# Last layer of a four-layer graph network on one core: where two transposes stand among a block's products, and which block's sum a block's gathers wait for

## The chip, the cores and the metric

The kernel runs on one core of a Trainium2 chip. The metric is device time in microseconds (us) of one execution. The engines are PE (TensorE), DVE (VectorE), ACT (ScalarE), POOL (GpSimd) and SP (SyncE); DMA transfers are issued from SP, ACT and POOL.

## The reference: what is computed

Four graph layers run on 2708 nodes with 128 features, each as `x = layernorm(x + layer(x, adj))`, with one adjacency matrix of a few entries in each row. Only the last layer matters here:

```python
s = x @ msg_w[:, :D].T
d = x @ msg_w[:, D:].T
messages = gelu(s[:, None, :] + d[None, :, :] + msg_b)      # 2708 x 2708 x 128
aggregated = einsum('ijd,ij->id', messages, adj)
new = concat([x, aggregated]) @ upd_w.T + upd_b
h = gelu(new) + x
x = layernorm(x + layernorm(h) * ln_w + ln_b)
```

A message counts only where the adjacency has an entry. For a node i the sum therefore runs over its few neighbours j, and each of them needs row j of `d`.

## The kernel before

**Until the last layer.** The first three layers end with `TD` in DRAM, which holds the rows of `d` by node, and with lists that give each node its neighbours, sorted by degree. The nodes stand in 22 blocks of 128 (the last has 20). The change touches nothing of this.

**One block of the last layer.** A block has up to nine slots of neighbours. Six "pure" slots hold a neighbour for each of the 128 rows; three joined slots pack the rarer further neighbours of several rows together. The block with the 20 last nodes, block 21, has two slots in all. The functions, in `sparse_path`:

- `gathers(k)` (lines 1462 to 1479), on POOL: one indirect DMA for each slot (line 1467) brings 128 rows of `TD` into a tile `G`. Pure slots read their indices from `LP`, joined ones from `LM`, those of block 21 from `LT_`. There are four tiles `G`, used in turn (`ROWS`, line 1145).
- `terms(k)` (1481 to 1496): PE transposes the block's features and places them in the block's order, with two instructions into the PSUM tile `xT_ps` (1484 and 1485). ACT copies that to `xT` (1487), PE makes `sd_ps` (1489), DVE adds the bias to give `S` (1491), and PE spreads `S` to the joined slots as `q_ps` with JOIN products (1495).
- `weights(k)` (1498 to 1513), on DVE: ten tiles `W` of adjacency values.
- `messages(k)` (1515 to 1548): DVE adds `G` to `q_ps` and `S` (1539, 1542), and ACT takes the gelu (1546, 1547), giving `M`.
- `update(k)` (1550 to 1572), on PE, all from line 1557: products of the bias and of `xT`, then the **sum**, ten products `M` by `W` into one half of `af_ps`. ACT copies the sum to `aT` (1567). A last product of `aT` with `UB`, called the copy's product below, goes to the other half. ACT takes the gelu into `yo` (1572).
- `added(k)` and `norms(i)` (1579 to 1631), mostly on DVE: the residual, the two layer norms, and the store of the result from SP. `norms` runs once for a set of one to four blocks (`SETS`, 1388).

**The order.** `pinned` chains each instruction to the one before it on its engine, so every engine runs in the order in which the code emits. `ORDER` (1391) lists the blocks; block 21 stands eleventh, with index 10. The loop (1649 to 1667) goes over `ORDER`. In step n it emits the gathers and terms of block n+1, the messages of block n, the weights of block n+2, the update of block n, the residual of block n-1, and, when a set is full, its norms.

**The hold.** Since a gather needs only indices and a free tile, POOL could run far ahead. `HOLD = {0: 3}` (1460) makes the first gather of the block with index n, for n of 3 or more, wait for the instruction that `updated` names for the block three places back. `product` sets `updated[k]` at every call (1559), so it names the last one, the copy's product:

```python
if j in HOLD and n >= HOLD[j]:
    tc.add_manual_dep(
        i.ins, updated[ORDER[n - HOLD[j]]], ...
```

Of the kernel before, what the change touches and what calls it, by code (L numbers as in the profile page):

```python
# [25 lines left out]
F32 = mybir.dt.float32  # L26
# [11 lines left out]
P = 128  # L38
# [80 lines left out]
def sparse_path(  # L119
# [30 lines left out]
    NB = -(-N // P)  # L150
# [39 lines left out]
    ident = part["ident"]  # L190
# [20 lines left out]
    for h in range(HEADS):  # L211
        k = slice(h * HD, (h + 1) * HD)
# [49 lines left out]
    V_, S_, T_, G_ = nc.vector, nc.scalar, nc.tensor, nc.gpsimd  # L262
    newest = {}

    def pinned(i):

        e = i.ins.engine
        if e in newest:
            tc.add_manual_dep(
                i.ins, newest[e].name,  # L270
                mybir.DependencyInfo(mybir.DependencyClass.NoSync, mybir.DependencyReason.DATA),
                reason="order",
            )
        newest[e] = i.ins
        return i
# [102 lines left out]
    with (  # L378
# [49 lines left out]
        t = ps.tile([P, BANK], F32, name="tr_ps")  # L428
# [3 lines left out]
        t = ps.tile([P, 4, D], F32, name="hw_ps")  # L432
# [13 lines left out]
        t = ps.tile([P, BANK], F32, name="tr_ps")  # L446
# [5 lines left out]
        t = ps.tile([P, 4, D], F32, name="hw_ps")[:, 0, :2]  # L452
# [264 lines left out]
    with (  # L717
# [234 lines left out]
        def weights(k):  # L952
            pinned(S_.activation(HS[:, k, :], HS[:, k, :], AF.Copy, scale=DS[:, k : k + 1]))
# [162 lines left out]
    PLACE = late.tile([P, NB, P], F32, name="PLACE")  # L1116
    PLACE = late.tile([P, NB, P], F32, name="PLACE")
# [6 lines left out]
    X3 = late.tile([P, NB, D], F32, name="X3")  # L1124
# [55 lines left out]
    with (  # L1180
# [16 lines left out]
        t = ps.tile([P, BANK], F32, name="tr_ps")  # L1197
# [148 lines left out]
        for t in ROWS:  # L1346
            n = NG - WHOLE
# [43 lines left out]
    ORDER = [b for bs in SETS for b in bs]  # L1391
    with (
# [52 lines left out]
        def slots(k):  # L1445

            if k == NB - 1:
                return range(NT)
            if k == LAST:
                return (*range(PURE - 1), *range(PURE, NG), PURE - 1)  # L1450
            return range(NG)

        def source(k, s):

            if k == NB - 1:
                return LT_[:, s : s + 1]
            return LP[:, k, s : s + 1] if s < PURE else LM[:, k, s - PURE : s - PURE + 1]

        updated = {}
        HOLD = {0: 3}  # L1460

        def gathers(k):
            n = ORDER.index(k)
            G = Gs[k] = ROWS[ORDER.index(k) % len(ROWS)]
            for j, s in enumerate(slots(k)):
                bound = {"bounds_check": NP - 1, "oob_is_err": False} if s >= WHOLE else {}
                i = G_.indirect_dma_start(  # L1467
                    G[:, s, :], None, TD, bass.IndirectOffsetOnAxis(ap=source(k, s), axis=0),
                    **bound,
                )  # L1470
                if j in HOLD and n >= HOLD[j]:
                    tc.add_manual_dep(
                        i.ins, updated[ORDER[n - HOLD[j]]],
                        mybir.DependencyInfo(
                            mybir.DependencyClass.Sync, mybir.DependencyReason.DATA
                        ),
                        reason="no further ahead of the updates",
                    )
                pinned(i)

        def terms(k):

            t = ps.tile([P, 2 * P], F32, name="xT_ps")
            pinned(T_.transpose(t[:, :P], X3[:, k, :], ident))
            pinned(T_.matmul(t[:, P:], X3[:, k, :], PLACE[:, k, :], start=True, stop=True))
            xT = sb.tile([P, 2 * P], F32, name="xT")
            pinned(S_.copy(xT, t))
            m = ps.tile([P, 2 * D], F32, name="sd_ps")
            pinned(T_.matmul(m, xT[:, P:], W3[:, : 2 * D], start=True, stop=True))  # L1489
            S = sb.tile([P, 2 * D], F32, name="S")  # L1490
            pinned(V_.tensor_tensor(S, m, MB, ALU.add))  # L1491
            js = range(NM, NM + NT) if k == NB - 1 else range(NM)
            q = ps.tile([P, NM, D], F32, name="q_ps")
            for i, j in enumerate(js):
                pinned(T_.matmul(q[:, i, :], JOIN[:, j, :], S[:, :D], start=True, stop=True))  # L1495
            mids[k] = S, q, xT
# [18 lines left out]
        def messages(k):  # L1515
            S, q, xT = mids[k]
            G = Gs.pop(k)
            M = Ms[k] = wp.tile([P, NG + 1, D], F32, name="M")
            if k == LAST:
                last = PURE - 1  # L1520
                pinned(S_.activation(M[:, NG, :], S[:, D:], AF.Gelu))
                pinned(V_.tensor_tensor(
                    M[:, :last, :], G[:, :last, :],
                    S[:, :D].unsqueeze(1).to_broadcast([P, last, D]), ALU.add,
                ))
                pinned(S_.activation(M[:, :last, :], M[:, :last, :], AF.Gelu))
                yield
                pinned(V_.tensor_tensor(M[:, PURE:NG, :], G[:, PURE:, :], q, ALU.add))
                pinned(S_.activation(M[:, PURE:NG, :], M[:, PURE:NG, :], AF.Gelu))
                yield  # L1530
                pinned(V_.tensor_tensor(M[:, last, :], G[:, last, :], S[:, :D], ALU.add))
                pinned(S_.activation(M[:, last, :], M[:, last, :], AF.Gelu))
                return
            if k == NB - 1:
                n = NT
                pinned(V_.tensor_tensor(M[:, :n, :], G[:, :n, :], q[:, :n, :], ALU.add))
            else:
                n = NG
                pinned(V_.tensor_tensor(  # L1539
                    M[:, PURE:n, :], G[:, PURE:n, :], q, ALU.add  # L1540
                ))
                pinned(V_.tensor_tensor(  # L1542
                    M[:, :PURE, :], G[:, :PURE, :],
                    S[:, :D].unsqueeze(1).to_broadcast([P, PURE, D]), ALU.add,
                ))
            pinned(S_.activation(M[:, NG, :], S[:, D:], AF.Gelu))
            pinned(S_.activation(M[:, :n, :], M[:, :n, :], AF.Gelu))  # L1547
            yield

        def update(k):  # L1550
            order = slots(k)
            i, j = place[k]
            M, W, xT = Ms.pop(k), Ws.pop(k), mids.pop(k)[2]
            t = ps.tile([P, 2 * P], F32, name="af_ps")

            def product(to, a, b, start=False, stop=False):
                i = T_.matmul(to, a, b, start=start, stop=stop, skip_group_check=True)  # L1557
                pinned(i)
                updated[k] = i.ins.name

            product(t[:, P:], ONES, BIAS, start=True)
            product(t[:, P:], xT[:, :P], W3[:, 2 * D :])
            product(t[:, :P], M[:, NG, :], W[:, NG, :])
            for s in order:
                product(t[:, :P], M[:, s, :], W[:, s, :], stop=s == order[-1])
            aT = sb.tile([P, P], F32, name="aT")
            pinned(S_.copy(aT, t[:, :P]))  # L1567
            product(t[:, P:], aT, UB, stop=True)
            if not j:
                ys[i] = op.tile([P, 4, D], F32, name="yo")  # L1570
                sums[i] = op.tile([P, 4, 2], F32, name="mv")
            pinned(S_.activation(ys[i][:, j, :], t[:, P:], AF.Gelu))
# [6 lines left out]
        def added(k):  # L1579
            i, j = place[k]  # L1580
            h = ys[i][:, j, :]
            pinned(V_.tensor_tensor(h, h, X3[:, k, :], ALU.add))
            stats(sums[i][:, j, :], h)
# [49 lines left out]
        def some(steps, n=None):  # L1633
            for _ in islice(steps, n):
                pass
# [13 lines left out]
        for n, k in enumerate(ORDER):  # L1649
            if n + 1 < NB:  # L1650
                gathers(ORDER[n + 1])
                terms(ORDER[n + 1])
            steps = messages(k)
            next(steps)
            if n + 2 < NB:
                weights(ORDER[n + 2])
            if n + 1 < NB:
                update(k)
                if n:
                    added(ORDER[n - 1])  # L1660
                i, j = place[k]
                if n and not j:
                    before = norms(i - 1)
                    if n + 2 < NB:
                        some(before)
                    else:
                        some(before, 22)
# [3 lines left out]
        i = len(SETS) - 1  # L1671
        first, second = norms(i - 1), norms(i)
        next(first)
        some(steps)
        some(first, 4)
        update(LAST)
        added(LAST)
        next(second)
# [525 lines left out]
```

## Time and profile before

| What | us |
|---|---|
| median of 6 runs | 647.01 |
| lowest and highest of them | 644.87 and 650.72 |
| the profiled execution | 646.7 |
| its span, first to last instruction | 644.9 |
| last layer's gathers, first start to last end | 371.76 to 626.96 |
| after the last gather | 17.9 |

Busy time of the engines over the whole span is 469.1 us on PE (73%), 455.4 on DVE, 374.6 on POOL and 220.0 on ACT. Over the gathers of the last layer, 371.7 to 627.0, it is 150.1 on PE, 163.7 on DVE, 53.3 on ACT and 197.3 on POOL, at a mean PE clock of 0.79 of full speed. The DMA engines are busy for 0.20 of that stretch.

In the lines of the profile, a group reads: line, engine, operation, tile written and tiles read, count, then busy us, mean ns of one, idle us of the engine just before and what ended it. "issue" means that the profile shows nothing that the engine waited for. A line in order of time reads: start, duration, engine, line, operation, and in brackets the idle time before it.

### The profile page before, as it was taken

Reading aid. Unit: us, or ns where it says so; the run is one execution under the profiler, and the core shown is the slowest. Engines: PE = TensorE matmul, PEld = TensorE weight load, DVE = VectorE, ACT = ScalarE, POOL = GpSimd, SP = SyncE. Lnnn points to the kernel's source line nnn. Section 1 sums busy time; section 2 is a strip of 40 time slices with the busy share of each in tenths; the row PEclk is TensorE's granted clock in tenths of the full one; section 3 lists DMA queues with packets and bytes.
Section 4 is the critical chain, followed back from the end, with each engine's and each line's share of the span. In section 5 each row is a group of like instructions: output and inputs, shape, how many; then the busy total and the mean of one; then the engine's idle time right before and its main releaser. Section 6 shows DMA issues by size and latency. Waiting matters only on the chain.

```text
span 644.9 us, 8660 instructions
## 1 busy us (share of the span) xinstructions
PE 469.1 (73%) x2795; PEld 324.2 (50%) x2795; DVE 455.4 (71%) x1300; ACT 220.0 (34%) x518; POOL 374.6 (58%) x473
## 2 busy tenths in 40 slices
PE   6779999997949996999784647754745754755651
PEld 5745444664425432466584636544645644644641
DVE  3766999999998999271746556539439675575863
ACT  4025656685234000059615722211212212112120
POOL 6102113253577677346377477777777777777770
PEclk9569999999888999999756756977977969769695
DMA  9988999999699999768312311112112122121220
GB/s 304 378 343 316 405 424 405 394 349 397 252 388 371 394 382 412 290 197 218 102 43 48 92 35 48 45 46 60 46 44 63 47 52 47 45 60 45 55 51 15
DMA packets 46886, 124.29 MB, mean 193 GB/s; under 512 B 10303, under 2 KB 25077, under 8 KB 40559
## 3 DMA queue, kind: packets, MB, share of 16 engines
q0 software_dynamic: 15200, 69.06, 30.3%
q1 hardware_dynamic: 25230, 51.28, 22.3%
q10 hardware_dynamic: 6400, 3.30, 1.9%
q8 instruction: 24, 0.39, 0.3%
q14 instruction: 32, 0.25, 0.1%
HBM read 118.55 MB, written 6.30 MB: 194 GB/s over the span
## 4 chain that ended last, share of the span: by engine, by line
POOL 30%; PE 23%; DMA 15%; issue 14%; DVE 12%; ACT 3%; SPq 1%; POOLq 0%; DVEq 0%; ACTq 0%
POOL G L1467 20%; PE acc L878 18%; DMA G<-TD,LP 4%; DMA TOP<-in_high 4%; POOL ga L1190 3%; DMA ah<-in_adjR 2%; DVE VI L655 2%; POOL HS L948 2%; DMA ah<-in_adjL,PERM 2%; PE z L974 1%; DMA G<-TD,LM 1%; POOL ah L853 1%; DVE cand L642 1%; DMA TH<-H 1%; POOL TL L600 1%
## 5 line engine op out<-in xcount | busy, mean ns | idle before, releaser
L1467 POOL DMA_INDIRECT G<-TD,LP x126 | 131.6, 1044 | 44.5 <-issue 34.1
L878 PE MATMUL acc<-ah,XD 128*128 128x512 f32 (+1 forms) x264 | 113.8, 569 | 1.0 <-ACT XD L746 1.0
L1557 PE MATMUL af_ps<-W,M 128*128 128x128 f32 x426 | 77.1, 349 | 42.5 <-ACT M L1547 39.8
L655 DVE FIND_INDEX8 VI<-VI,nat 128x8 uint32<-128x2707 f32 x34 | 100.8, 2972 | 0.0
L1557 PEld LDWEIGHTS af_ps<-W,M 128*128 128x128 f32 x426 | 71.9, 260 | 45.9 <-ACT M L1547 42.8
L1467 POOL DMA_INDIRECT G<-TD,LM x63 | 63.8, 1012 | 19.2 <-issue 18.9
L985 ACT ACTIVATE sign<-ah 128x1536 bf16<-128x1536 f32 (+1 forms) x44 | 58.2, 1328 | 44.1 <-issue 27.0
L878 PEld LDWEIGHTS acc<-ah,XD 128*128 128x128 f32 x264 | 47.9, 196 | 44.7 <-issue 42.4
L878 PE MATMUL acc<-ah,HS 128*128 128x512 f32 x132 | 64.9, 629 | 6.9 <-DMA ah<-in_adjL,PERM 6.0
L1547 ACT ACTIVATE M<-M 128x1152 f32<-128x1152 f32 (+1 forms) x21 | 23.7, 1128 | 101.0 <-DVE M L1542 99.6
L1495 PE MATMUL q_ps<-S,JOIN 128*128 128x128 f32 x130 | 25.1, 340 | 37.6 <-DVE S L1491 37.6
L621 POOL DMA_INDIRECT nat<-in_adjo,PERM x22 | 21.9, 997 | 45.8 <-issue 19.6
L1491 DVE TENSOR_TENSOR S<-sd_ps,MB 128x256 f32<-128x256 f32 x22 | 9.3, 421 | 53.9 <-PE sd_ps L1489 53.9
L878 PEld LDWEIGHTS acc<-ah,HS 128*128 128x128 f32 x132 | 25.8, 202 | 38.3 <-issue 36.7
L1495 PEld LDWEIGHTS q_ps<-S,JOIN 128*128 128x128 f32 x130 | 20.2, 232 | 47.1 <-DVE S L1491 47.1
L635 DVE MAX8 VI<-nat 128x8 f32<-128x2707 f32 x12 | 35.6, 2968 | 1.4 <-DMA nat<-in_adjo,PERM 1.4
L642 DVE MAX8 cand<-nat 128x8 f32<-128x338 f32 (+3 forms) x96 | 34.8, 437 | 2.4 <-DMA nat<-in_adjo,PERM 2.4
L1507 DVE TENSOR_SCALAR W<-TAB,LL 128x128 f32<-128x128 f32 x126 | 34.0, 356 | 0.0
L1190 POOL DMA_INDIRECT ga<-TA,TOPJ x22 | 24.5, 1114 | 10.4 <-issue 6.4
L1567 ACT COPY aT<-af_ps 128x128 f32<-128x128 f32 x22 | 5.9, 266 | 70.0 <-PE af_ps L1557 70.0
L1539 DVE TENSOR_TENSOR M<-G,q_ps 128x384 f32<-128x384 f32 x20 | 11.0, 548 | 25.8 <-DMA G<-TD,LM 25.7
L974 PEld LDWEIGHTS <-sign 128*128 128x128 bf16 x484 | 18.0, 96 | 18.8 <-issue 8.2
(337 smaller groups left out, 948.4 us busy)
## 6 DMA issues: line engine op xcount, KB each, us to landing
ah<-in_adjL SPq DMA_DIRECT2D x22, 768.0 KB, 14.1
ah<-in_adjR SPq DMA_DIRECT2D x44, 330.0 KB, 5.1
TOP<-in_high SPq DMA_DIRECT2D x5, 1408.0 KB, 17.5
ah<-in_adjL SPq DMA_DIRECT2D x22, 256.0 KB, 8.2
G<-TD,LP POOLq DMA_INDIRECT x126, 2.6
TA<-XD ACTq DMA_DIRECT2D x5, 264.0 KB, 3.7
TH<-H ACTq DMA_DIRECT2D x5, 256.0 KB, 10.2
G<-TD,LM POOLq DMA_INDIRECT x63, 2.5
```

The lines of the kernel that those rows point to most:

```text
L635: pinned(nc.vector.max(V[:, b, 0:8], t))
L642: pinned(nc.vector.max(c[:, 8 * k : 8 * k + 8], t[:, at]))
L655: pinned(nc.vector.max_index(IX[:, b, s], V[:, b, s], t))
L878: pinned(T_.matmul(acc[i][:, :w], weights[:, n, :], a[:, i * BANK : i * BANK + w], start=n == 0, stop=n == NB - 1,))
L974: pinned(T_.matmul(z[:, i, :], m[:, blk(i)], F4[:, n, :], start=n == 0 and i == 0, stop=n == NB - 1, skip_group_check=True,))
L985: pinned(S_.activation(m[:, : hi - lo], a, AF.Sign))
L1190: pinned(G_.indirect_dma_start(ga[:, i, :], None, TA, bass.IndirectOffsetOnAxis(ap=TOPJ[:, b : b + 1], axis=0)))
L1467: i = G_.indirect_dma_start(G[:, s, :], None, TD, bass.IndirectOffsetOnAxis(ap=source(k, s), axis=0), **bound,)
L1495: pinned(T_.matmul(q[:, i, :], JOIN[:, j, :], S[:, :D], start=True, stop=True))
L1507: pinned(V_.tensor_scalar(W[:, s, :], part["lane"], to, v, ALU.is_equal, ALU.mult))
L1547: pinned(S_.activation(M[:, :n, :], M[:, :n, :], AF.Gelu))
L1557: i = T_.matmul(to, a, b, start=start, stop=stop, skip_group_check=True)
```

## The change

It has three parts. The two transposes of `terms` become a function `turn`. `update` of the block with index n calls it for the block with index n+2, between the last product of the sum and the copy of the sum, so that they stand ahead of the copy's product on PE; `terms` then begins with ACT's copy. `updated[k]` now names the last product of the sum, not the copy's product. And for index n over 4 the first gather waits for the block two places back, not three. The blocks with index 0 and 1 are still turned in their `terms`; the updates of the last two blocks turn nothing.

```diff
                 if j in HOLD and n >= HOLD[j]:
                     tc.add_manual_dep(
-                        i.ins, updated[ORDER[n - HOLD[j]]],
+                        i.ins, updated[ORDER[n - HOLD[j] + (n > 4)]],
...
-        def terms(k):
-
-            t = ps.tile([P, 2 * P], F32, name="xT_ps")
+        turned = {}
+
+        def turn(k):
+
+            t = turned[k] = ps.tile([P, 2 * P], F32, name="xT_ps")
             pinned(T_.transpose(t[:, :P], X3[:, k, :], ident))
             pinned(T_.matmul(t[:, P:], X3[:, k, :], PLACE[:, k, :], start=True, stop=True))
+
+        def terms(k):
+
+            if k not in turned:
+                turn(k)
             xT = sb.tile([P, 2 * P], F32, name="xT")
-            pinned(S_.copy(xT, t))
+            pinned(S_.copy(xT, turned.pop(k)))
...
-        def update(k):
+        def update(k, ahead=None):
...
                 pinned(i)
-                updated[k] = i.ins.name
+                return i
...
             for s in order:
-                product(t[:, :P], M[:, s, :], W[:, s, :], stop=s == order[-1])
+                i_ = product(t[:, :P], M[:, s, :], W[:, s, :], stop=s == order[-1])
+            updated[k] = i_.ins.name
+            if ahead is not None:
+                turn(ahead)
             aT = sb.tile([P, P], F32, name="aT")
             pinned(S_.copy(aT, t[:, :P]))
...
-                update(k)
+                update(k, ORDER[n + 2] if n + 2 < NB else None)
```

## The prediction

> **What bounds the kernel now.** I read the page's busy shares and chain first, then the instructions of POOL and ACT in order of time through the last layer, because the diff touches nothing ahead of it. On the page, part 4 and the first group of part 5:
>
> ```profile
> POOL 30%; PE 23%; DMA 15%; issue 14%; DVE 12%; ACT 3%; SPq 1%; POOLq 0%; DVEq 0%; ACTq 0%
> ...
> L1467 POOL DMA_INDIRECT G<-TD,LP x126 | 131.6, 1044 | 44.5 <-issue 34.1
> ```
>
> The gathers of line 1467 are the largest piece of the chain. The view of waits for POOL from 372 to 627 us says what they wait for:
>
> ```profile
> POOL G L1467 <- issue: 53.7, 176, 0.3
> POOL G L1467 <- DMA TD<-YD: 6.4, 1, 6.4
> POOL G L1467 <- DMA G<-TD,LP: 2.7, 9, 0.3
> POOL G L1467 <- DVE M L1539: 0.9, 3, 0.3
> ```
>
> The columns are total us, times, longest us. After the 6.4 us ahead of the first gather no wait is longer than 0.3 us, the ordinary distance of two gathers, and PE does not appear: **the hold on the sum three blocks back never ends a wait.** From 371.76 to 626.96 POOL issues 191 gathers without a pause, nine to a block (two for the short block 21), about 12 us a block. PE, DVE and ACT follow it. What makes POOL pause therefore comes out at the end in full, and what makes PE faster is worth nothing until it reaches POOL.
>
> Call p a block's place in ORDER, 0 to 21. The short block is p=10. The change makes the first gather of p wait for the last product of sum p-2 (p from 5). To see whether that wait binds, I set two times side by side: when POOL gets to that gather (in order of time on POOL), and when sum p-2 ends (ACT's copy aT starts 0.04 us later). Around the short block, first POOL, then ACT:
>
> ```profile
> 492.72 0.96 POOL L1467 DMA_INDIRECT G<-TD,LT__3106  x1 [0.30 <-issue]
> 493.98 0.96 POOL L1467 DMA_INDIRECT G<-TD,LT__3106  x1 [0.30 <-issue]
> 495.25 0.95 POOL L1467 DMA_INDIRECT G<-TD,LP  x1 [0.31 <-issue]
> ...
> 507.43 0.96 POOL L1467 DMA_INDIRECT G<-TD,LP  x1 [0.30 <-issue]
> ```
>
> ```profile
> 488.72 0.27 ACT L1567 COPY aT<-af_ps 128x128 f32<-128x128 f32 x1 [3.75 <-PE af_ps L1557]
> ...
> 502.14 0.27 ACT L1567 COPY aT<-af_ps 128x128 f32<-128x128 f32 x1 [3.96 <-PE af_ps L1557]
> ...
> 507.05 0.27 ACT L1567 COPY aT<-af_ps 128x128 f32<-128x128 f32 x1 [1.37 <-PE af_ps L1557]
> ```
>
> Column one is the start, two the duration, the bracket the idle time before. Block p=10 has two gathers, so POOL is at p=11 at 495.25, only 2.5 us after it began p=10. Sum 9, which p=11 would now wait for, is copied at 502.14. In before it waited for block 8, whose copy stands at 488.72.
>
> **The change, part by part.** (1) The hold from p=5 on. Gather start less copy of p-2, in us, p=5 to 21: 3.7, 4.1, 2.1, 5.6, 3.7, 4.0, **-6.9**, 0.4, 4.4, 1.6, 5.6, 3.7, 4.1, 1.7, 5.6, 3.7, 3.3. One is negative. Sum 9 will not come earlier: its adds on DVE (495.58) stand behind the norms of p=4 to 7, which keep DVE without a gap from 485.33 to 495.24, then come the gelu and 18 products from 498.24 to 502.10. None of that is touched.
>
> Size of the pause: PE frees ACT at 502.14. No gather of this layer waits for PE in the trace; the nearest rows are L1593 on POOL, which begins 0.09 us after DVE's mv ends (627.50 after 627.41), the 0.30 us of issue ahead of every gather, which may or may not lie under the wait. So it starts at 502.2 to 502.5, a pause of 6.95 to 7.25; I take 7.1, the middle. A gather after a long idle took 1.10 (at 371.76) where 0.95 is usual: +0.1. Against it, the gathers of p=11 lay beside the weights of DVE (496.9 to 499.6) and two took 1.31 and 1.18; those 0.5 us go, but p=12 (9 gathers in 8.89 us busy against 9.44 for p=11) now meets the adds and weights of p=11: about even, the sum of these is 0 within 0.5. Queued behind the waiting gather on POOL are the other eight of p=11, all 90 of p=12 to 21, and the three small pairs L1593/L1594 of the last norms; DVE's adds of each block wait for them. No DMA of SP or ACT stands behind it but the stores of the results, which move with their norms.
>
> Is the pause paid back? POOL has no other wait to lose, so only through shorter gathers (a rival below). Does it set off others? Last gather of p=11 at 506.11+7.1=513.2; adds 2.6 later (p=8: 479.74 to 482.35) at 515.8, where they stood at 509.73; sum 11 takes 6.4 more (p=8: 482.35 to 488.72), 522.2, and p=13 asks for it at 526.2. DVE's norms and sum 12 move by 6.1 to 535.8; p=14 asks at 538.4. Further on both sides move alike and keep their distances. After the last gather 17.9 us follow (626.96 to 644.9) which move as a whole.
>
> A rule on the PE clock bears on sum 11. Rows first: after 4.70 us of idle PE took 1.22 us for four JOIN products at 495.71, and 0.94 for six at 504.96; a sum's 18 products take 2.27 us or up to 4.21. The Trainium skill ("TensorE: Matmul & The Clock Gate", What's actually happening) says that PE falls to half its clock after an idle window of about 3.4 us, which speaks against a pause: PE would then idle some 7 us before sum 11. By rule and row alike that costs up to 1.9 us there; 522.2 already has the slow 3.7 to 4 us in it, and 4.0 us are free.
>
> (2) The holds of p=3 and 4 move from the product with UB to the sum ahead of it: both were done 9 to 14 us before (399.84 and 407.49 against 409.17 and 421.07). Nothing.
>
> (3) The transposes of p+2, for 20 blocks, move from behind the product with UB to the gap before it. They fill 502.78 to 503.28, 0.50 us, and the gap is 0.35 us long (PE idle before the UB product). But the copy xT behind them waits for none of this: it starts at 503.31 with no idle, straight after ACT's gelu of yo (502.98), which waits for the UB product. PE's next product (503.74) starts 0.06 after that copy ends. So nothing is gained on this chain, and UB may come 0.15 us later (0.65 on the slow clock, the 0.50 doubled). Bounds over 20 blocks, if PE were the bound: 10 us less (20 x 0.50) to 13 more. I take 0, since in this layer PE waits 35.6 us for S ahead of the JOIN products and 9.3 for xT while POOL runs through; p=12's distance to sum 10, the one that such a delay reaches, grows from 0.4 to 7.5 by the pause.
>
> Sum: 646.7 (profiled execution: span 644.9 and 1.8 around it) + 7.1 + 0 + 0 = **653.8 us**. The median before is 647.0, 0.3 above that execution; this is 1.0% over it.
>
> **Rivals.** *Shorter pause*: with the slots of sum 9 at the quick clock, 2.27 instead of 3.86 us, the pause is 5.5 and the time 652.2. For it: the transposes shift PE's work by half a microsecond. Against: the 4.70 us of idle before 495.71 come from DVE's norms. Chance 0.10.
>
> *More holds bind*: p=7, 14 and 18 have 2.1, 1.6 and 1.7 us, all after a norms pass. If each loses its distance and up to 1.5 more, 4.5 us are added: 658.3. Against: sums 12 and 16 had the slow clock already. Chance 0.08.
>
> *Not slower*: the pause shifts gathers against DVE's work. The shortest gathers are 0.94 (LP) and 0.99 us (LM); 99 of them, from 495.2 to 627, would take 94.8 busy us, and took 101.8 (9.44 and 92.39 in the view of stretches). If all 7.0 us went, the time would be 646.8; over 3.9 must go to come within 0.5%. The long ones stand beside DVE (1.55 at 524.09, where the adds run from 523.82 to 524.77), and DVE's adds start when a block's gathers land, so the phase comes back by itself. Chance 0.06. The Trainium skill ("SBUF — State Buffer", Who interferes with whom) has DVE and GpSimd share one port pair that the first holds for its whole instruction, but infers that two-input adds leave descriptor writing alone; by it that 1.55 needs another cause, and the sum stays as it is.
>
> *The hold changes nothing and the transposes gain*: if POOL's wait were already met, and PE's chain the bound, 10 us less, 637; without the gain 647. POOL's row of waits speaks against both. Chances 0.03 and 0.01.
>
> **Numbers.** Forecast 653.8, own range 652.2 to 655.5, chance 0.72. Range 650.5 to 657.5: it takes in the shorter pause and most of the further holds, and leaves out what is not slower. What a measurement tells from no change is 0.5%, 3.2 us: faster is below 643.8, slower above 650.2. Faster 0.03, same 0.07, slower 0.90.
>
> **What would show it.** On POOL one idle time of about 7 us before the first LP gather behind the two LT gathers, released by PE's af_ps sum, at about 502, and no other above 0.5; the last gather ending near 634 with 18 us behind it; PE's two transposes ahead of UB, with xT's copy still straight after yo's gelu. Wrong if sum 9 ends before 499, if three or more holds bind, or if the mean gather falls by over 0.03 us.

## The result, and the profile after the change

The changed kernel takes 652.14 us (median of 20 runs, 647.61 to 658.72) against 647.01 for the kernel before (46 runs beside them, 643.92 to 655.38). The ratio is 1.0076, 95% interval 1.0059 to 1.0093: 5.1 us slower, and the whole interval lies above the 0.5% that a measurement can tell from no change. The profiled execution took 653.87 us with a span of 652.0; that of before took 646.7 with 644.9. The two spans differ by 7.1 us, the medians by 5.1.

The chain that ended last, and the first group of the costliest instructions, of the changed kernel:

```profile
PE 26%; POOL 25%; issue 15%; DVE 14%; DMA 12%; ACT 3%; SPq 1%; POOLq 0%; DVEq 0%; ACTq 0%
...
L1467 POOL DMA_INDIRECT G<-TD,LP x126 | 131.1, 1040 | 51.8 <-issue 35.4
```

POOL has fallen from 30 to 25% of the chain and PE has risen from 23 to 26%. The gathers themselves are as they were (131.1 us for 126 of them, 131.6 before); what has grown is the idle time just ahead of them, 44.5 to 51.8 us. The view of POOL's waits from 360 to 640 us (total us, times, longest us) says where those 7.3 us stand:

```profile
POOL G L1467 <- issue: 54.9, 180, 0.3
POOL G L1467 <- PE af_ps L1564: 7.6, 1, 7.6
POOL G L1467 <- DMA TD<-YD: 6.3, 1, 6.3
```

The second row is new. It is one wait, not several. In order of time on POOL, around the short block (the two LT gathers), and then on ACT:

```profile
493.02 0.96 POOL L1467 DMA_INDIRECT G<-TD,LT__3106  x1 [0.31 <-issue]
494.29 0.96 POOL L1467 DMA_INDIRECT G<-TD,LT__3106  x1 [0.30 <-issue]
502.84 0.94 POOL L1467 DMA_INDIRECT G<-TD,LP  x1 [7.60 <-PE af_ps L1564]
504.09 0.94 POOL L1467 DMA_INDIRECT G<-TD,LP  x1 [0.31 <-issue]
```

```profile
489.19 0.27 ACT L1577 COPY aT<-af_ps 128x128 f32<-128x128 f32 x1 [3.90 <-PE af_ps L1564]
...
502.61 0.27 ACT L1577 COPY aT<-af_ps 128x128 f32<-128x128 f32 x1 [4.12 <-PE af_ps L1564]
...
507.35 0.27 ACT L1577 COPY aT<-af_ps 128x128 f32<-128x128 f32 x1 [1.37 <-PE af_ps L1564]
...
522.53 0.27 ACT L1577 COPY aT<-af_ps 128x128 f32<-128x128 f32 x1 [4.30 <-PE af_ps L1564]
...
534.69 0.27 ACT L1577 COPY aT<-af_ps 128x128 f32<-128x128 f32 x1 [2.91 <-PE af_ps L1564]
```

POOL is done with the short block at 495.25 and would go on at 495.54. It goes on at 502.84, 0.23 us after ACT has begun to copy sum 9. The view of stretches, of after and then of before, cut at the first gather, at the pause and at the last gather, gives the whole balance (start and end, length, then busy us and instructions of PE, PEld, DVE, ACT and POOL, the granted clock, DMA):

```profile
372.28:495.54 123.26, 70.25 (x369) 60.10 (x369) 75.83 (x263) 25.16 (x58) 95.23 (x92) 0.78 0.19 47
495.54:502.84 7.30, 6.80 (x31) 6.38 (x31) 4.99 (x17) 1.40 (x2) 0.00 (x0) 0.54 0.19 47
502.84:634.00 131.16, 78.91 (x421) 68.75 (x420) 83.00 (x316) 24.43 (x59) 101.29 (x99) 0.78 0.19 49
634.00:652.00 18.00, 2.91 (x11) 2.28 (x10) 6.54 (x28) 1.38 (x4) 2.41 (x7) 0.54 0.09 23
```

```profile
371.76:495.25 123.49, 69.52 (x369) 58.84 (x369) 75.76 (x264) 26.17 (x58) 95.44 (x93) 0.78 0.19 46
495.25:626.96 131.71, 80.45 (x451) 69.35 (x451) 87.91 (x333) 27.07 (x60) 101.82 (x99) 0.81 0.21 52
626.96:644.90 17.94, 2.90 (x11) 2.29 (x10) 6.52 (x28) 1.38 (x4) 2.40 (x6) 0.53 0.09 24
```

Line by line: the layer starts 0.52 later (372.28 against 371.76, ahead of anything that was changed), the first eleven blocks take 0.23 less, the pause adds 7.30, the 99 gathers behind it take 0.55 less (131.16 against 131.71), the tail 0.06 more. The sum is 7.10, the difference of the spans.

### The profile page after: what moved, and what is told of

The parts are those of the page before. It is cut to its first block, busy times and chain, and to the rows that moved or that the text cites. A ratio compares the mean times of both kernels' runs of the same rounds, so it can differ in the third digit from the quotient of the medians.

```text
span 652.0 us, 8659 instructions
## 1 busy us (share of the span) xinstructions
PE 474.8 (73%) x2795; PEld 330.8 (51%) x2795; DVE 455.5 (70%) x1300; ACT 217.4 (33%) x518; POOL 373.3 (57%) x473
## 4 chain that ended last, share of the span: by engine, by line
PE 26%; POOL 25%; issue 15%; DVE 14%; DMA 12%; ACT 3%; SPq 1%; POOLq 0%; DVEq 0%; ACTq 0%
PE acc L878 19%; POOL G L1467 18%; DMA TOP<-in_high 4%; DVE VI L655 3%; POOL ga L1190 3%; DMA ah<-in_adjR 2%; DMA G<-TD,LP 2%; DMA ah<-in_adjL,PERM 2%; DVE VI L635 2%; PE z L974 1%; PE af_ps L1564 1%; DMA G<-TD,LM 1%; DVE cand L642 1%; POOL TL L600 1%; SPq L388 1%
## 5 line engine op out<-in xcount | busy, mean ns | idle before, releaser
L1467 POOL DMA_INDIRECT G<-TD,LP x126 | 131.1, 1040 | 51.8 <-issue 35.4
L1564 PE MATMUL af_ps<-W,M 128*128 128x128 f32 x426 | 81.1, 362 | 48.4 <-ACT M L1554 45.6
L1564 PEld LDWEIGHTS af_ps<-W,M 128*128 128x128 f32 x426 | 75.7, 272 | 51.8 <-ACT M L1554 48.7
```

Source lines behind the costliest of these rows:

```text
L1467: i = G_.indirect_dma_start(G[:, s, :], None, TD, bass.IndirectOffsetOnAxis(ap=source(k, s), axis=0), **bound,)
```

## The experiments

The theory: the one pause at p=11, which the hold makes, is the whole loss, and the transposes are worth nothing while POOL bounds the layer. The rivals: the transposes take part in it (by an earlier or later sum), or further holds bind as well. Each experiment is an edit of the kernel before or of the changed one.

**The hold alone.** The kernel before, with the hold's new distance and the product that it now waits for, and the transposes where they were:

```diff
-                        i.ins, updated[ORDER[n - HOLD[j]]],
+                        i.ins, updated[ORDER[n - HOLD[j] + (n > 4)]],
...
-                updated[k] = i.ins.name
+                return i
...
-                product(t[:, :P], M[:, s, :], W[:, s, :], stop=s == order[-1])
+                i_ = product(t[:, :P], M[:, s, :], W[:, s, :], stop=s == order[-1])
+            updated[k] = i_.ins.name
```

> The new hold alone, the transposes left where they were in before. Theory (one pause of about 7 us at index 11 is the whole change, the transposes are worth nothing): as the changed kernel, 5 to 7 us over before (652 to 654), with one idle time of 7 to 7.6 us of POOL ahead of a gather. Rival (the transposes give about 2 us back, which is why the medians lie 5.1 apart and the profiled spans 7.1): 654 or more, about 2 us over the changed kernel.

Measured: 651.88 us (10 runs) against 646.81, ratio 1.0081 (1.005 to 1.0113). Its one wait of the gathers for PE's sums:

```profile
POOL G L1467 <- PE af_ps L1557: 7.2, 1, 7.2
```

The hold alone has the changed kernel's loss and the changed kernel's pause.

**The transposes alone.** The transposes moved as in the change, with the hold three blocks back as before. The hold waits here for the last product of the sum, as in the changed kernel, and no longer for the product with UB:

```diff
+        turned = {}
...
+        def turn(k):
...
+            t = turned[k] = ps.tile([P, 2 * P], F32, name="xT_ps")
...
-                updated[k] = i.ins.name
+                return i
...
+            updated[k] = i_.ins.name
+            if ahead is not None:
+                turn(ahead)
...
-                update(k)
+                update(k, ORDER[n + 2] if n + 2 < NB else None)
```

> The transposes moved and the hold's event moved to the end of the sum, but all holds three blocks back. Theory: as before, 647, within 1.5 us either way; no gather waits for PE. Rival (the transposes give 2 us back): 645, below before in the interval.

Measured: 646.63 us (12 runs), ratio 1.0009 (0.9981 to 1.0038), span 644.8. No gather waits for PE. The transposes (and the earlier event of the hold) neither cost nor bring anything that shows here.

**Every hold but that at p=11**, and **that at p=11 alone**, both in the changed kernel:

```diff
-                        i.ins, updated[ORDER[n - HOLD[j] + (n > 4)]],
+                        i.ins, updated[ORDER[n - HOLD[j] + (n > 4 and n != 11)]],
```

```diff
-                        i.ins, updated[ORDER[n - HOLD[j] + (n > 4)]],
+                        i.ins, updated[ORDER[n - HOLD[j] + (n == 11)]],
```

> The changed kernel, but the gather with index 11 waits three blocks back as in before; the other 16 wait two back. Theory: as before, 647, within 1.5 us, and no gather waits for PE, since the other distances are 0.4 us or more. Rival (further holds bind now and then, at index 7, 12, 14 or 18): 1.5 us or more over before, with waits on PE at those blocks.

> The changed kernel, but only the gather with index 11 waits two blocks back. Theory: as the changed kernel, 5 to 7 us over before, one idle time of 7 to 7.6 us. Rival (the other holds share the cost): clearly under the changed kernel, 649 to 650.

Measured: without it 646.98 us (12 runs), ratio 1.0001 (0.9976 to 1.0026); it alone 654.12 us (6 runs), ratio 1.014 (1.0103 to 1.0177). POOL's waits, first of the kernel without the hold at p=11, where no gather behind the first waits longer than the ordinary 0.3 us, then of the kernel with that hold alone:

```profile
POOL G L1467 <- issue: 53.9, 177, 0.3
POOL G L1467 <- DMA TD<-YD: 6.3, 1, 6.3
...
POOL G L1467 <- DVE M L1546: 0.9, 3, 0.3
POOL G L1467 <- PE af_ps L1564: 0.3, 1, 0.3
```

```profile
POOL G L1467 <- issue: 54.0, 177, 0.3
POOL G L1467 <- PE af_ps L1564: 7.5, 1, 7.5
```

In the first of them one row names PE: the first gather of p=12, whose distance the prediction had at 0.4 us, begins after 0.32 us of idle, where 0.30 is usual. So that hold is met, but only just, and it costs nothing.

One hold of the seventeen is the loss. But with it alone the time is 7.3 us over before, and with all of them 5.1, and the intervals of the two ratios do not meet. The theory has nothing that would give 2 us back, since the other holds end no wait above 0.32 us in any of these profiles. So the kernel with p=11 alone was run twice more.

**The hold at p=11 alone once more**, first beside the changed kernel:

> The changed kernel once more, beside the next one, which differs only in holds that end no wait. The theory has no place for a difference between the two: both 5 to 7.3 us over before, their intervals overlapping. Rival (the other 16 holds, though never waited for in a profile, give about 2 us back): this one again about 2 us under the next.

> The changed kernel with the new hold at index 11 alone, once more. Theory: as the changed kernel within 1.5 us. Rival: 2 us over it again (7.3 over before).

Those two, and the two of the next experiment, ran on a chip on which the kernel before took 694.92 us (23 runs) in place of 647. There the changed kernel took 684.13 (6 runs), ratio 0.987 (0.9806 to 0.9934), **faster** than before, and the hold at p=11 alone 696.9 (12 runs), ratio 1.0045 (1.0007 to 1.0084). That is no answer to the question, and a finding of its own, told below. On a further chip, with 646.53 us for the kernel before:

> The changed kernel, with the hold of two blocks back at index 11 alone and three back from index 12 on. Theory (the pause at index 11 is the whole loss, the holds behind it end no wait): on a chip where the kernel before takes about 647 us it has the changed kernel's time, 5 to 7.3 us above the kernel before (ratio 1.0075 to 1.0113), one wait of the gathers on PE of 7 to 7.6 us, and its interval of ratios overlaps the changed kernel's 1.0059 to 1.0093. Rival (the later holds, though no profile shows them ending a wait, give some 2 us back, so that the hold at index 11 alone costs more than all of them): again a ratio above 1.0105, clear of the changed kernel's. If the chip is one on which PE's signals come late, the ratio tells neither.

Measured: 653.2 us (6 runs), ratio 1.0109 (1.0075 to 1.0143), a pause of 7.5. This interval meets that of the changed kernel (1.0059 to 1.0093) as well as that of the first measurement. The theory's number is met and the rival's "clear of the changed kernel's" is not, but 6.7 us is nearer to 7.3 than to 5.1: a return of 1 to 2 us through the other holds is not excluded. In the profiled executions 0.5 to 0.8 us of it can be seen: from the first gather's start to the last one's end it is 261.72 us in the changed kernel and 261.63 with the hold alone, but 262.42 and 262.21 in the two with p=11 alone. These are single executions.

**The short block elsewhere.** The short block goes from the third place of its set to the end of the next one, so that the block behind it (now p=15) asks for another sum; once with the holds of before, once with the change.

```diff
-        (0, 1, 2, 3), (4, 5, 6, 7), (8, 9, NB - 1), (10, 11, 12, 13), (14, 15, 16), (17, 18),
+        (0, 1, 2, 3), (4, 5, 6, 7), (8, 9, 10), (11, 12, 13, NB - 1), (14, 15, 16), (17, 18),
```

> Before, with the short block from index 10 to index 14, at the end of the set 11, 12, 13 (sets of 3 and 4 in place of 3 and 4). Holds three back. Theory: POOL issues the same 191 gathers without a pause, 647 within 2 us. It is the partner of the next one.

> The changed kernel with the short block at index 14. Theory (POOL outruns the sum two back wherever a block has two gathers): no wait at index 11 and one at index 15; the sum two back ends 7.5 to 9 us after the last long gather of its own block, POOL is there after 3.9, so a pause of 3.5 to 5.5 us and as much over its partner. Rival (the pause belongs to the place, behind the norms of the first eight blocks): a wait still near index 11 or 12, none at 15.

Measured, on the chip with 694.92 us for before: 694.81 (10 runs, ratio 1.0027, 0.9993 to 1.0061) and 684.39 (4 runs, ratio 0.9886, 0.9831 to 0.9941). Inconclusive: at p=15 POOL pauses 5.47 us with the change, but 6.94 without it, among a dozen pauses in either. What the move does on a chip like the others wasn't tried.

**No hold at all**, in the kernel before:

```diff
-        HOLD = {0: 3}
+        HOLD = {}
```

> Before without any hold: a gather waits only for its tile to be read, four blocks back. Theory (the hold three back ends no wait): as before, 647 within 1.5 us. Rival (the hold three back does something that the waits do not show, as pacing): over 2 us off.

Measured: 647.55 us (10 runs) against 646.04, ratio 1.0033 (1.0004 to 1.0061); the profiled execution had a span of 642.2, and no gather waits for PE. The hold three back, which ends no wait, is worth at most some 0.6% and perhaps nothing. The profiled execution is the fastest of its ten, and not because of its gathers: they began at 369.12, 2.64 us sooner than in the kernel before, and then took 256.11 us from the first start to the last end, 255.20 before.

**POOL's cover taken away.** If the transposes are worth nothing only because POOL bounds the layer, a kernel with fewer gathers should show their worth. The gathers of before, cut to four a block, so that a part of the messages is left out; once with the transposes where they were and once moved. As above, the second kernel's hold waits for the last product of the sum, three blocks back, the first one's for the product with UB:

```diff
-            for j, s in enumerate(slots(k)):
+            for j, s in enumerate(list(slots(k))[:4]):
```

> Before, with the first four gathers of each block alone; the rest of a tile keeps old rows, so part of the messages is left out. POOL then needs some 5 us a block and the chain over PE, ACT and DVE sets the pace. Partner of the next; some 50 to 80 us under before.

> The same with the transposes moved ahead of the copy's product, holds three back; the same part is left out. Theory (xT's copy stands behind yo's gelu on ACT, so the moved transposes shorten nothing even where POOL no longer covers them): within 2 us of its partner. Rival (they were worth 0.50 us a block, hidden by POOL alone): about 10 us less than its partner.

Measured: 609.66 us (4 runs, ratio 0.9444, 0.9407 to 0.9481) and with the transposes moved 610.4 (4 runs, ratio 0.9455, 0.9405 to 0.9504). POOL is the bound no more: it now waits for PE at most of the holds, as its waits show, first with the transposes behind UB, then ahead of it:

```profile
POOL G L1467 <- PE af_ps L1557: 73.5, 14, 11.8
```

```profile
POOL G L1467 <- PE af_ps L1564: 82.3, 15, 11.0
```

Two blocks on ACT in the first of these kernels, then two in the second:

```profile
509.09 0.27 ACT L1567 COPY aT<-af_ps 128x128 f32<-128x128 f32 x1 [3.56 <-PE af_ps L1557]
...
516.74 0.27 ACT L1567 COPY aT<-af_ps 128x128 f32<-128x128 f32 x1 [2.37 <-PE af_ps L1557]
517.59 0.28 ACT L1572 ACTIVATE yo<-af_ps 128x128 f32<-128x128 f32 x1 [0.58 <-PE af_ps L1557]
517.92 0.37 ACT L1487 COPY xT<-xT_ps 128x256 f32<-128x256 f32 x1
```

```profile
511.30 0.27 ACT L1577 COPY aT<-af_ps 128x128 f32<-128x128 f32 x1 [3.82 <-PE af_ps L1564]
...
518.78 0.27 ACT L1577 COPY aT<-af_ps 128x128 f32<-128x128 f32 x1 [2.37 <-PE af_ps L1564]
519.63 0.28 ACT L1582 ACTIVATE yo<-af_ps 128x128 f32<-128x128 f32 x1 [0.58 <-PE af_ps L1564]
519.80 0.37 ACT L1494 COPY xT<-xT_ps 128x256 f32<-128x256 f32 x1
```

From one sum's copy to the next it is 7.65 us (516.74 less 509.09), and 7.48 with the transposes moved (518.78 less 511.30): 0.17 us a block, the same 0.17 by which xT's copy follows the gelu of yo sooner (0.33 us from start to start, then 0.17). So there is a gain, and it is small: at most 20 x 0.17 = 3.4 us. It isn't seen in the time. The steps from the last block of a set to the first of the next grew: 15.03, 13.25, 14.55, 15.26 and 14.64 us became 15.33, 14.26, 14.97, 15.71 and 15.05, 2.6 us more in all, where the other 16 steps gave back 3.1. Of the third of them 0.26 is the set's first sum on a slower clock (3.96 us for 20 products at a granted clock of 0.59, 3.70 at 0.63 in the other kernel), 0.11 the norms on DVE; why the others grew stays open. Besides, the profiled execution of the second kernel began its last layer 2.53 us later (373.92 against 371.39), ahead of anything that differs; from there to its end it took 234.98 us, the first 235.71.

## Why the prediction held, step by step

- **POOL bounds the layer, and one hold of the seventeen binds.** Right, and shown from both sides: without the hold at p=11 the loss is gone (1.0001), with it alone the loss is there (1.014, 1.0109).
- **The pause, 7.1 us (6.95 to 7.25).** 7.60 us of idle, of which 0.30 are ahead of every gather: 7.30 in the changed kernel, 0.05 above the stated bounds, and 6.9 to 7.2 in the three others (7.2, 7.5 and 7.5 less 0.3). POOL began 0.23 us after ACT did; the prediction had put that at 0.06 to 0.36. POOL also got to p=11 0.23 us sooner than in the kernel before, counted from the first gather (123.26 us against 123.49).
- **Shorter or longer gathers behind it, 0 within 0.5.** 0.55 us less for the 99 gathers: the bound was missed by a hair. One term did not come: the first gather behind the pause took 0.94 us, not the 1.10 of a gather after a long idle. Nor do the long gathers go with what the prediction named. It set them beside DVE's adds (the 1.55 us at 524.09) and, on the Trainium skill's rule that such adds leave descriptor writing alone, said that another cause was needed. Here it is, in the profile of before, first on POOL, then on DVE:

```profile
524.09 1.55 POOL L1467 DMA_INDIRECT G<-TD,LP  x1 [0.30 <-DVE M L1539]
```

```profile
524.69 1.61 DVE L1507 TENSOR_SCALAR W<-TAB,LL 128x128 f32<-128x128 f32 x6
```

0.6 us after that gather began, DVE went over from the adds to the weights, a TENSOR_SCALAR with one input. Sorted by what runs on DVE beside them, the LP gathers of the kernel before took 0.96 us beside adds without weights (20 of them, none above 1.2), 0.98 beside nothing (24, none) and 1.10 beside weights (52, of which 15 above 1.2). The other 30, beside other work of DVE, have one above 1.2. So the rule ("SBUF — State Buffer", Who interferes with whom) agrees with these rows; it also counts TENSOR_SCALAR among the operations that can take the shared port pair, under conditions that no run here tests. Of the 7.0 us that the prediction called the excess of the last 99 gathers, the 28 LP gathers beside weights make up 5.1 (31.45 us in all, against 0.94 each). The sorting is a reading of one trace; no run took the weights away.
- **Later holds keep their distance.** The copies of sums 11 and 12 stand at 522.53 and 534.69 (worked out: 522.2 and 535.8), and p=13 and p=14 came 3.7 us after each (4.0 and 2.6). p=12 came 7.0 us after sum 10 (7.5). PE idled 6.68 us ahead of sum 11, and its 18 products took 4.21 us, as the row from before had it.
- **The holds of p=3 and 4, nothing.** No wait at either.
- **The transposes, 0.** The time is right (1.0009 alone); the step was not quite. It read xT's copy, at 503.31 without idle time behind a gelu that ended at 503.26, as released by that gelu. The transposes ended at 503.28, and it was they that held it: moved ahead of UB they let the copy follow the gelu by 0.17 us in place of 0.33, from start to start. Nor did UB come later, for which the prediction had allowed 0.15 us: it follows the start of the sum's copy by 0.31 us (502.61 to 502.92), 0.32 before (502.14 to 502.46). In the changed kernel the product with W comes 1.43 us after the start of the sum's copy (502.61 to 504.04), 1.60 before (502.14 to 503.74). That is "nothing gained on this chain" mis-sized by 0.17 us a block, hidden here by POOL as the step said of the rest.
- **The sum.** 653.8 was worked out for the profiled execution and 653.87 is what it took. So close a match is luck: the later start (0.52) and the longer pause (0.2) were given back by the first eleven blocks (0.23) and the gathers behind the pause (0.55), and the executions of the changed kernel lie between 647.61 and 658.72. The median is 1.7 us lower, just below the prediction's own range (652.2 to 655.5) and inside the wider one (650.5 to 657.5): the loss is 5.1 us by the medians (3.8 to 6.0 by the interval), less than the 7.3 of the pause. The four kernels with the pause lost 5.1, 5.1, 7.3 and 6.7 us by their medians. Where an execution wins back one or two of them stays open. The gathers behind the pause are a candidate (0.55 in the profiled one). Another is PE's clock at sum 9: in the profiled execution with the transposes alone the last 18 products took 2.86 us at a granted clock of 0.78, and the copy came 129.25 us after the first gather began (500.53 less 371.28); in the changed kernel they took 4.03 at 0.54, and the copy came after 130.33. An execution of the changed kernel with the quicker sum would, by this estimate, pause 1.1 us less. No run tells how often that happens.
- **The rivals.** *Shorter pause*: not in the profiled execution, where sum 9's 18 products took 4.03 us (3.87 before) and its copy came 130.33 us after the first gather began (130.38 before); in other executions it may be so, as just said. *More holds bind*: none did; that of p=12 was the nearest to it, without the hold at p=11. *Not slower*: the gathers gave back 0.55 of the 3.9 us that this needed. On these chips it is refuted; on one chip the sign did turn, by another mechanism, which none of the rivals had.

## What to carry to other kernels

A wait that is to hold a queue back costs nothing until one place falls short. So set, for each place, the time at which the queue gets there beside the time at which the awaited result is ready, and look first at the odd-sized item: a short block brings the queue to the next item early, and a wait counted in blocks then reaches much less far in time. On the engine that bounds the stage the shortfall comes out at the end in full or nearly so. And an operation that starts within some hundredths of a microsecond after two others have ended may wait for either, so compare both ends before a move of one of them is put at zero.

## What the runs showed that was not expected

On one chip of those used the kernel before took 694.92 us in place of 647, and the change made it faster (684.13). Up to the first gather of the last layer everything was as elsewhere (it began at 370.9 in the changed kernel there, at 372.28 here). The time went in the last layer, and not into the engines' work (over the span PE was busy for 475.9 us there and 474.8 here, DVE for 455.0 and 455.5, POOL for 376.0 and 373.3). The first sum there, on PE, ACT and POOL of the changed kernel:

```profile
394.91 4.02 PE L1564 MATMUL af_ps<-W,M 128*128 128x128 f32 x20
398.76 0.27 PE L1486 MATMUL xT_ps<-TAB,X 128*128 128x128 f32 x1
398.87 0.39 PE L1487 MATMUL xT_ps<-PLACE,X 128*128 128x128 f32 x2
411.05 0.80 PE L1564 MATMUL af_ps<-UB,aT 128*128 128x128 f32 x2 [11.79 <-ACT aT L1577]
```

```profile
410.73 0.27 ACT L1577 COPY aT<-af_ps 128x128 f32<-128x128 f32 x1 [15.64 <-remote]
```

```profile
406.93 1.00 POOL L1467 DMA_INDIRECT G<-TD,LM  x1 [0.30 <-issue]
410.96 0.96 POOL L1467 DMA_INDIRECT G<-TD,LP  x1 [3.04 <-remote]
```

By this record, which models the ends of PE's products, PE had ended the sum at 398.93 and gone on to the transposes. ACT, idle till then, began to copy it at 410.73, 11.8 us later; in every profile from the other chips it is 0.04 us, at all 22 sums. Added up over the 22 blocks the delay is 66 us in the changed kernel there and 82 in the one with the short block moved and the old holds. Not ACT alone was late: POOL's held gather, which waits for the same products, went on 0.23 us after ACT. What came late is PE's signal: the trace has PE's semaphore step at 410.70, where in the kernel with the hold alone, on another chip, it steps at 399.71 for a sum that ended at 399.70. It came 2.8 us after the last gather that POOL could issue ahead of its hold had ended (407.93). In the kernel with the short block moved it was the same: sum 0 ended at 399.06, ACT began at 412.10, and POOL's last gather ahead of the hold had ended at 409.29, 2.8 us before. At later sums that came late this distance varies, from about 0 to 3.4 us. A hold two blocks back stops POOL nine gathers sooner at most places, and there the signal seems to get through sooner; that would be why the change, and the short block with it (0.9886), gain 10 us there and the hold at p=11 alone doesn't (1.0045). The four traces from that chip agree with it: the delays add up to 66 us in each of the two kernels with the hold two blocks back, to 79 with p=11 alone and to 82 with the old holds. But that is only read from traces, in which about two thirds of the semaphore steps of the gathers' landings aren't recorded, and no experiment took it apart. What holds the signal back on that chip, and whether a small part of it plays on the others, where the records show no such delay, stays open.
